# Graph attention and two GCN layers on one core: first loads, checks, result loads, quotients and the order of the last stages rewritten

## The chip, the cores and the metric

The kernel runs on one core of a Trainium2 chip. The metric is device time in microseconds (us) of one execution of the whole program; lower is better. Three executions of the kernel before took 6879.35, 6883.69 and 6887.78 us, so the median is 6883.69 us.

## The reference

The input is x with N = 2708 rows and D = 128 features, and a sparse matrix adj of 2708 x 2708. Everything is float32. With H = 8:

```python
q = (x @ Wq.T).reshape(d, n, h)            # k and v in the same way; d = 128 attentions of width 8
a = einsum('dnh,dmh->dnm', q, k) * scale + adj + adj
out = einsum('dnm,dmh->dnh', softmax(a, axis=2), v).reshape(n, h * d)
x = layernorm(x + out @ Wo.T)
local_hidden = adj @ (x @ W2) + b2
local_cross = adj @ (local_hidden @ W4) + b4
x = layernorm(x + local_cross + local_hidden @ res_w.T + res_b)
```

So there are 128 attentions over 2708 x 2708 positions, each with the same doubled adj added to its scores, and then two products with adj, each reading all of its 29.3 MB.

## The kernel before, in words

**Attention.** Four of the 128 attentions form a group (GB = 4, 32 partitions each), so there are 32 groups g. The query columns are cut into six blocks of 452 (the last has 448), and the key rows into 22 chunks of 128, of which the last is short. For each group and block a plan of nine steps is written out by hand (`interleave`), 1728 steps in all, and the engines run it in that order (`tc.manual_schedule()`, line 313). In a step TensorE forms scores into PSUM (line 438), VectorE adds the adj tile (line 445), ScalarE takes the exponentials (lines 534 and 537), and GpSimd multiplies one chunk's exponentials by exponentials of adj (line 535). TensorE then sums the weighted values (line 463). Projections of x into keys, queries and values go to DRAM (`ks`, `qs`, `vs`) and are read back group by group. Keys and queries are each stored as a high and a low part of 8 rows, so that a group's four attentions occupy 4 x 32 partitions. The sums, eight numerators and one denominator for each position, go to DRAM as `os_`.

**The start.** Lines 369 to 375 load x, the three projection weights and two adj tiles. The first key tile of group 0 comes by 16 transfers of 8 rows (line 254), alternating between the queues of SyncE (SP) and ScalarE, and its queries by 8 transfers of 16 rows (line 287). Line 407 loads the input of the first projection that stands inside the attention.

**Checks.** The attention takes no maxima; a later check decides whether they were needed. `first_exp` (line 413) takes the exponential of adj once in group 0, writes it to DRAM, and has ScalarE add up its elements (`accum_out`). `look_at_near` (line 423) reduces such a tile to its minimum on VectorE, in the last three groups alone. `divide` keeps the smallest and the largest denominator (line 598), and a block at line 652 reduces all these to one number, `n_fine`. After everything, `rest` reads that number (line 721), and a second path runs only if it says so.

**Layer 0's end** (`layer0_out`, line 579). It works on 22 chunks c of 128 rows in an order that is written out. `load(c)` brings a 576 KB tile `ot` of numerators and denominators and a 64 KB tile `xt` of x. `divide(c)` multiplies by reciprocals on VectorE (lines 595 and 600), TensorE transposes eight times (line 603), ScalarE copies. `project(c-1)` multiplies by Wo (line 611), and `add_x(c-2)` adds x and takes statistics. Both load tiles have three buffers. The weights are loaded before this stage (lines 543 to 550). Afterwards the rows are normalised, transposed and multiplied by W2 (lines 632 to 651).

**Layer 1** (`layer1`, line 669). `propagate` sums 22 products of 128 rows into one column block of 512 (six blocks, the last of 148). Each product takes one adj tile of 256 KB from a pool of 24 buffers. The first pass (from line 686) adds b2 and multiplies by W4; the second (from line 694) adds the residual, transposes four pieces, normalises each, and stores each with a transfer on SP's queue (line 705). Here the instructions' order was not written out: a scheduler placed them, and it also placed adj loads of this stage among the loads of layer 0's end.

All loads and stores but the first few stand in one queue, SP's, which issues them in order. SP waits at a transfer until the data or the buffer it needs is there.

Of the kernel before, what the change touches and what calls it, by code (L numbers as in the profile page):

```python
# [9 lines left out]
F32 = mybir.dt.float32  # L10
# [8 lines left out]
P = 128  # L19
# [11 lines left out]
NEAR_LOW = 1e-30  # L31
NEAR_HIGH = 1e18
# [110 lines left out]
def graph_attention_gcn(ctx: ExitStack, tc: tile.TileContext, x, xT, adj, adjT, adjP, adjS,  # L143
# [42 lines left out]
    ends = const.tile([P, 2, len(QBS) * len(TWO_EXP)], F32, name="ends")  # L186


    with ExitStack() as s:
# [58 lines left out]
        def load_keys(g, h, queue=nc.sync):  # L248


            if h == 0:
                groups[g] = kpool.tile([P, NU, P], F32R, tag="k", name="k"), k_short[g % 2], vals[g % 2], v_short[g % 2]
                raw_keys[g] = raw.tile([P, N], F32R, tag="k_raw", name="k_raw")
            queue.dma_start(raw_keys[g][ds(H * h, H), :].bitcast(F32),
                              ks[ds(H * (h % 4 // 2), H), ds((GB * g + h // 4) * N, N)])
# [26 lines left out]
        def load_q(g, b, queues=(nc.sync, nc.sync)):  # L282
            n0, nw = QBS[b]
            q = queries[g, b] = qpool.tile([P, QB], F32R, tag="q", name="q")
            for j in range(GB):
                for i in range(2):
                    queues[i].dma_start(q[ds(32 * j + 2 * H * i, 2 * H), :nw].bitcast(F32),  # L287
                                      qs[:, ds((GB * g + j) * N + n0, nw)])
# [85 lines left out]
        for n in range(2):  # L374
            load_adj(n)

# [20 lines left out]
        for h in range(16):  # L397
            load_keys(0, h, nc.scalar if h % 2 else nc.sync)
# [8 lines left out]
        load_quarter(0)  # L407
# [5 lines left out]
        def first_exp(b, m):  # L413

            nw = QBS[b][1]
            t = ecols.tile([P, QB], F32, tag="ecol", name="ecol")
            x = b * len(TWO_EXP) + TWO_EXP.index(m)
            nc.scalar.activation(t[:, :nw], adj_cols[0, b, -1 - m][:, :nw], AF.Exp, scale=2.0,
                                 accum_out=ends[:, 1, x : x + 1])
            nc.sync.dma_start(near_exp[b, m][:, :nw], t[:, :nw])  # L420
            exp_cols[0, b, m] = t

        def look_at_near(g, b, m):

            x = TWO_EXP.index(m)
            if x % 3 == g - NG + 3:
                nc.vector.tensor_reduce(ends[:, 0, ds(b * len(TWO_EXP) + x, 1)], exp_cols[g, b, m][:, : QBS[b][1]],
                                        AX.X, ALU.min)
# [51 lines left out]
        for what, n, c, beside in interleave(plan, len(steps) // len(plan), NU, amid, bufs=5):  # L480
# [14 lines left out]
            if c == 1 and jobs:  # L495
                jobs.pop(0)()
            if c == 0:
                nq = (g, b + 1) if b + 1 < len(QBS) else (g + 1, 0)
                if i == 3 and nq[0] < NG:
                    load_q(*nq)  # L500

                if g + 1 < NG:
                    t = b * len(plan) + i
                    if t < 32 and t % 2 == 0:
                        load_keys(g + 1, t // 2)
                    elif t < 32 and t % 8 == 7:
                        load_values(g + 1, t // 8)
                    elif 33 <= t < 50 and t % 2:
                        order_keys(g + 1, (t - 33) // 2)
                    elif t >= 50:  # L510
                        spread_values(g + 1, t - 50)
                last = max(loads.index((g, b, x), max(0, loaded - 40)) for x in [chunks_of(p) for p in pieces] + [-1 - two])
                while loaded < min(len(loads), last + 1 + ahead):
                    load_adj(loaded)
                    loaded += 1
                e = epool.tile([P, 8, QB], F32, tag="e", name="e")
                sp = pq.tile([P, 3, NB], F32, tag="p", name="p")
                w = ppool.tile([P, 3, QB], F32, tag="w", name="w")
                if g == 0:
                    first_exp(b, two)  # L520
                at = k = 0
# [10 lines left out]
            if c == len(pieces) - 1:  # L532
                look_at_near(g, b, two)
                nc.scalar.activation(w[:, :, :nw], sp[:, :, :nw], AF.Exp, scale=2.0)  # L534
                nc.gpsimd.tensor_mul(w[:, :, :nw], w[:, :, :nw],  # L535
                                     exp_cols[g, b, two][:, :nw].unsqueeze(1).to_broadcast([P, 3, nw]))
                nc.scalar.activation(e[:, :at, :nw], e[:, :at, :nw], AF.Exp, scale=2.0)  # L537
# [5 lines left out]
    wo = keep.tile([P, H, D], F32, name="wo")  # L543
    nc.sync.dma_start(wo.rearrange("g e f -> g (e f)"), WoT)
    w2, w4, rw = (keep.tile([P, P], F32, name=f"w{i}") for i in range(3))
    for t, src in ((w2, W2), (w4, W4), (rw, res_wT)):
        nc.sync.dma_start(t, src)
    b2_sb, b4_sb, rb_sb, bias = (keep.tile([P, 1], F32, name=f"b{i}") for i in range(4))
    for t, src in ((b2_sb, b2), (b4_sb, b4), (rb_sb, res_b)):
        nc.sync.dma_start(t, src)  # L550
    nc.vector.tensor_add(bias, b4_sb, rb_sb)

# [8 lines left out]
    reach = keep.tile([P, 2, NM], F32, name="reach")  # L561
    nc.gpsimd.memset(reach, 1.0)
    fine = keep.tile([P, 5], F32, name="fine")
# [15 lines left out]
    def layer0_out(sb, ps, pa, judge):  # L579
# [4 lines left out]
        def load(c):  # L584
            i0, w = MC[c]
            ot = sb.tile([P, H + 1, P], F32, tag="ot", name="ot")
            nc.sync.dma_start(ot[:w], o3[ds(i0, w)])
            xt = sb.tile([P, D], F32, tag="xt", name="xt")
            nc.sync.dma_start(xt[:w], x[ds(i0, w), :])
            given[c] = ot, xt  # L590

        def divide(c):
# [3 lines left out]
            if judge:  # L596
                for i, op in enumerate((ALU.min, ALU.max)):
                    nc.vector.tensor_reduce(reach[:w, i, c : c + 1], ot[:w, H, :], AX.X, op)
            on = sb.tile([P, H, P], F32, tag="on", name="on")
            nc.vector.tensor_mul(on[:w], ot[:w, :H, :], rd[:w].unsqueeze(1).to_broadcast([w, H, P]))  # L600
# [17 lines left out]
        load(0)  # L618
        load(1)
        for c in range(NM + 2):  # L620
            if c + 2 < NM:
                load(c + 2)
# [29 lines left out]
        if judge:  # L652
            finite = sb.tile([P, NM * D], F32, tag="finite", name="finite", bufs=1)
            nc.vector.tensor_scalar(finite, ys.rearrange("p c f -> p (c f)"), 0.0, 0.0, ALU.mult, ALU.is_equal)
            nc.vector.tensor_reduce(fine[:, 0:1], finite, AX.X, ALU.min)
            bounds = [(reach[:, 0, :], ALU.min, SUM_LOW, ALU.is_ge), (reach[:, 1, :], ALU.max, SUM_HIGH, ALU.is_le)]
            bounds += [(ends[:, 0, :], ALU.min, NEAR_LOW, ALU.is_ge), (ends[:, 1, :], ALU.max, NEAR_HIGH, ALU.is_le)]
            for i, (a, way, limit, op) in enumerate(bounds):
                end = keep.tile([P, 1], F32, name=f"end{i}")
                nc.vector.tensor_reduce(end, a, AX.X, way)  # L660
                nc.vector.tensor_scalar(fine[:, 1 + i : 2 + i], end, limit, None, op)
            every, ones = (keep.tile([P, 1], F32, name=n) for n in ("every", "ones"))
            nc.vector.tensor_reduce(every, fine, AX.X, ALU.min)
            nc.gpsimd.memset(ones, 1.0)
            pf = pa.tile([P, NB], F32, tag="py", name="pf", bufs=2)
            nc.tensor.matmul(pf[:1, :1], every, ones, start=True, stop=True)
            nc.vector.tensor_copy(n_fine, pf[:1, :1])

    def layer1(s, cols):
# [4 lines left out]
        def propagate(src, n0, nw, last=None):  # L674

            acc = ps.tile([P, NB], F32, tag="wide", name="acc1")
            for m, (m0, mw) in enumerate(MC):
                t = cols.tile([P, NB], F32, tag="col", name="col1")
                nc.sync.dma_start(t[:mw, :nw], adjT[ds(m0, mw), ds(n0, nw)])
                nc.tensor.matmul(acc[:, :nw], src[:mw, m, :], t[:mw, :nw], start=(m == 0),  # L680
                                 stop=(last is None and m == NM - 1))
            if last is not None:
# [3 lines left out]
        for n0, nw in NBS:  # L686
            acc = propagate(xw, n0, nw)
            nc.vector.tensor_scalar(lhT[:, ds(n0, nw)], acc[:, :nw], b2_sb, None, ALU.add)
            for i, w in chunks(nw, P):
# [4 lines left out]
        for n0, nw in NBS:  # L694
            acc = propagate(hw, n0, nw, (rw, lhT[:, ds(n0, nw)]))
            eT = sb.tile([P, NB], F32, tag="eT", name="eT")
            nc.vector.tensor_scalar(eT[:, :nw], acc[:, :nw], bias, None, ALU.add)
            for i, w in chunks(nw, P):
# [7 lines left out]

    def rest(judge):
        with ExitStack() as s:
            cols = s.enter_context(tc.tile_pool(name="cols1", bufs=24))
            with ExitStack() as t:  # L710
# [3 lines left out]
                t.enter_context(tc.manual_schedule())  # L714
                layer0_out(sb, ps, pa, judge)
            layer1(s, cols)
# [136 lines left out]
```

## Time and profile before

| What | us |
|---|---|
| Median of three executions | 6883.69 |
| The profiled execution | 6884.26 |
| Its span, first to last instruction | 6882.5 |
| First score of the attention begins | 41.27 |
| Copy of the last sums begins (line 469) | 6542.98 |
| First and last reciprocal of layer 0's end begin (line 595) | 6553.02 and 6634.42 |
| First product with adj begins (line 680) | 6649.35 |
| Second pass over adj begins | 6764.71 |
| Sixth column block of the second pass begins | 6867.45 |
| Last result store is issued (line 705) | 6877.5 |

The times of single instructions are in us from the span's start. In a timeline line, the columns are start, length, engine, source line, operation, tile written and tile read, shapes, and count; "SPq" is a transfer issued by SP's queue, whose length is that of the issue and not of the transfer. A bracket tells how long the engine had been idle and what ended it. PE is TensorE's matmul stream, PEld its weight loads, DVE VectorE, ACT ScalarE, POOL GpSimd.

### The profile page before, as it was taken

The numbers are of one execution on the slowest core, as the hardware profiler recorded it, in microseconds if no ns is written. First come the engines' busy times: TensorE is split into PE (matmuls) and PEld (weight loads), VectorE is DVE, ScalarE is ACT, GpSimd is POOL, SyncE is SP. The second block draws the span as 40 slices with busy tenths as digits, with TensorE's granted clock in tenths as the row PEclk, the third lists the DMA queues.
The fourth block names the chain that finished last, engine by engine and source line by source line (L and its number), as shares of the span: only waits on it lengthen the run. The fifth ranks groups of instructions, "written<-read, shape, count | busy, mean of one in ns | idle before, by whom it ended". The sixth has DMA issues, their size and how long they took to land.

```text
span 6882.5 us, 138849 instructions
## 1 busy us (share of the span) xinstructions
PE 6655.3 (97%) x50666; PEld 2002.7 (29%) x50666; DVE 6106.7 (89%) x6373; ACT 6505.4 (95%) x3659; POOL 5789.3 (84%) x2706
## 2 busy tenths in 40 slices
PE   7999999999999999999999999999999999999979
PEld 2222222222222222222222222222222222222254
DVE  6899999999999999999999999999999999999941
ACT  7999999999999999999999999999999999999910
POOL 5899988989888899998889999889898898888800
PEclk8999999999999999999999999999999999999999
DMA  8888888778888877788887778887788878777667
GB/s 254 261 250 250 249 244 248 243 246 250 249 254 245 239 245 244 246 251 252 246 243 248 244 240 250 242 253 243 248 251 247 249 233 239 243 233 230 193 204 233
DMA packets 1168590, 1674.27 MB, mean 243 GB/s; under 512 B 153982, under 2 KB 1135954, under 8 KB 1163802
## 3 DMA queue, kind: packets, MB, share of 16 engines
q1 hardware_dynamic: 1167642, 1664.50, 79.0%
q8 instruction: 402, 6.59, 0.4%
q14 instruction: 290, 2.38, 0.1%
q10 hardware_dynamic: 256, 0.81, 0.1%
HBM read 1582.90 MB, written 81.80 MB: 242 GB/s over the span
## 4 chain that ended last, share of the span: by engine, by line
PE 58%; DMA 11%; DVE 11%; POOL 6%; issue 5%; ACT 5%; SPq 4%; DVEq 0%; ACTq 0%; POOLq 0%
PE acc L463 29%; PE s L438 18%; DVE e L445 10%; POOL w L535 6%; DMA col<-in_adjP 4%; PE acc L680 3%; DMA two<-in_adjP 3%; ACT e L537 3%; PE p L438 2%; PE acc L455 2%; SPq L287 2%; ACT w L534 2%; DMA ecol<-ne 2%; PE s L344 1%; PE acc L460 1%
## 5 line engine op out<-in xcount | busy, mean ns | idle before, releaser
L535 POOL TENSOR_TENSOR w<-w,ecol 128x1356 f32<-128x1356 f32 (+1 forms) x1728 | 5347.8, 3102 | 696.1 <-ACT w L534 601.6
L445 DVE TENSOR_TENSOR e<-s,col 128x904 f32<-128x904 f32 (+1 forms) x4608 | 4817.2, 1091 | 320.6 <-PE s L438 130.3
L537 ACT ACTIVATE e<-e 128x2712 f32<-128x2712 f32 (+5 forms) x1728 | 4593.8, 2658 | 9.3 <-DVE e L445 4.3
L463 PE MATMUL acc<-e,vals 128*9 128x452 f32 x20352 | 3561.9, 545 | 0.4 <-ACT e L537 0.4
L438 PE MATMUL s<-q,k 32*128 32x452 f32 x10944 | 2475.2, 462 | 120.9 <-DVE e L445 93.3
L534 ACT ACTIVATE w<-p 128x1356 f32<-128x1356 f32 (+1 forms) x1728 | 2286.0, 1323 | 33.9 <-PE p L438 20.4
L438 PEld LDWEIGHTS s<-q,k 32*128 32x128 f32 x10944 | 997.6, 182 | 3267.6 <-DVE e L445 2845.5
L463 PE MATMUL acc<-w,vals 128*9 128x452 f32 x10368 | 1622.0, 544 | 0.0
L438 PE MATMUL p<-q,k 32*128 32x452 f32 (+1 forms) x5184 | 1328.1, 444 | 21.2 <-ACT w L534 19.6
L445 DVE TENSOR_TENSOR e<-s,two 128x904 f32<-128x904 f32 (+1 forms) x960 | 1048.3, 1092 | 126.5 <-PE s L438 81.3
L463 PEld LDWEIGHTS acc<-e,vals 128*9 128x9 f32 x20352 | 441.7, 88 | 786.2 <-issue 773.7
L438 PEld LDWEIGHTS p<-q,k 32*128 32x128 f32 x5184 | 547.1, 182 | 51.0 <-ACT w L534 45.3
L463 PEld LDWEIGHTS acc<-w,vals 128*9 128x9 f32 x10368 | 207.0, 88 | 175.8 <-issue 160.3
L262 POOL CAST k<-k_raw 128x336 fp32r<-128x336 f32 x251 | 222.2, 886 | 30.1 <-DMA q<-qs 30.1
L460 PE MATMUL acc<-e,v_first 128*32 128x452 f32 (+1 forms) x1536 | 188.9, 564 | 9.8 <-DVE o L469 2.0
L455 PE MATMUL acc<-e,v_short 128*128 128x452 f32 (+1 forms) x384 | 195.1, 590 | 0.0
L344 PE MATMUL s<-wc,xc 128*128 128x256 f32 (+1 forms) x480 | 166.4, 428 | 8.9 <-DMA wc<-in_WkT 7.5
L469 DVE COPY o<-acc 128x452 f32<-128x452 f32 x192 | 119.9, 624 | 40.0 <-PE acc L463 39.8
L360 POOL TENSOR_TENSOR pr<-pa,pr 128x256 fp32r<-128x256 f32 (+1 forms) x160 | 117.8, 736 | 12.8
L346 DVE TENSOR_SCALAR pa<-s 128x256 f32<-128x256 f32 (+1 forms) x240 | 100.2, 418 | 27.6 <-PE s L344 23.9
L344 PEld LDWEIGHTS s<-wc,xc 128*128 128x128 f32 (+1 forms) x480 | 70.5, 184 | 133.4 <-DVE e L445 116.4
L680 PE MATMUL acc<-col,xw 128*128 128x512 f32 (+2 forms) x264 | 106.0, 551 | 0.0
(85 smaller groups left out, 1041.6 us busy)
## 6 DMA issues: line engine op xcount, KB each, us to landing
col<-in_adjP SPq DMA_DIRECT2D x1965, 226.0 KB
two<-in_adjP SPq DMA_DIRECT2D x1440, 226.0 KB
ecol<-ne SPq DMA_DIRECT2D x1395, 226.0 KB
col<-in_adjP SPq DMA_DIRECT2D x393, 224.0 KB
two<-in_adjP SPq DMA_DIRECT2D x288, 224.0 KB
ecol<-ne SPq DMA_DIRECT2D x279, 224.0 KB
col<-in_adjT SPq DMA_DIRECT2D x210, 256.0 KB
k_raw<-ks SPq DMA_DIRECT2D x504, 84.6 KB
```

Of the source, the lines that this page charges most:

```text
L262: copy(k[:, :, ts(i, n)], t[:, ts(i, n * NU)].rearrange("p (q c) -> p c q", c=NU))
L287: queues[i].dma_start(q[ds(32 * j + 2 * H * i, 2 * H), :nw].bitcast(F32), qs[:, ds((GB * g + j) * N + n0, nw)])
L344: nc.tensor.matmul(pp[:mi, 0, :QW], given[c][:, :mi], given.pop((c, i, h)), start=True, stop=True)
L438: nc.tensor.matmul(to[:, :nw], k[r, m, :], q[r], start=True, stop=True)
L445: nc.vector.tensor_add(e[:, ds(at, 2), :nw], st[:, :, :nw], a)
L455: nc.tensor.matmul(a[:, :nw], vz, e[:, t, :nw], start=False, stop=False)
L460: nc.tensor.matmul(a[ds(32 * j, 32), :nw], v_first[g % 2][:, ds(32 * j, 32)], e[:, t, :nw], start=True, stop=False)
L463: nc.tensor.matmul(a[ds(32 * j, VW), :nw], v[:, m, ds(VW * j, VW)], e[:, t, :nw], start=False, stop=(m == last_chunk))
L534: nc.scalar.activation(w[:, :, :nw], sp[:, :, :nw], AF.Exp, scale=2.0)
L535: nc.gpsimd.tensor_mul(w[:, :, :nw], w[:, :, :nw], exp_cols[g, b, two][:, :nw].unsqueeze(1).to_broadcast([P, 3, nw]))
L537: nc.scalar.activation(e[:, :at, :nw], e[:, :at, :nw], AF.Exp, scale=2.0)
L680: nc.tensor.matmul(acc[:, :nw], src[:mw, m, :], t[:mw, :nw], start=(m == 0), stop=(last is None and m == NM - 1))
```

## The change

At the start, keys of group 0 come by 8 transfers of 16 rows, and all its queries by transfers of 8 rows, 16 for each block, in the row order high, high, low, low. The first projection input inside the attention is loaded with the first loads. The sums by ScalarE and the minima by VectorE during the attention are gone; instead VectorE takes the largest absolute value of each adj tile in the first pass over adj, and the denominators are read again as one tile `sums`. The small weights are loaded 40 steps before the attention's end. In layer 0's end the loads are three chunks ahead (four buffers of `ot`, six of `xt`), and three of eight heads are multiplied by GpSimd. Layer 1 now lies in the written order too: pieces of a block's ending wait in a list `due` and are taken up at the products m = 3 and m = 6 of the next block. In the built program SP's queue therefore has, in the second pass, the four stores of a block right behind the adj tile m = 3 of the next block (m = 6 for the first), and all adj loads behind the loads of layer 0's end.

```diff
-    ends = const.tile([P, 2, len(QBS) * len(TWO_EXP)], F32, name="ends")
+    ends = const.tile([P, len(NBS) * NM], F32, name="ends")
+    nc.gpsimd.memset(ends, 0.0)
+    early = ctx.enter_context(tc.tile_pool(name="early", bufs=1))
...
+    def load_weights():
+        nc.sync.dma_start(wo.rearrange("g e f -> g (e f)"), WoT)
+        for t, src in ((w2, W2), (b2_sb, b2), (b4_sb, b4), (rb_sb, res_b)):
+            nc.sync.dma_start(t, src)
...
-            queue.dma_start(raw_keys[g][ds(H * h, H), :].bitcast(F32),
-                              ks[ds(H * (h % 4 // 2), H), ds((GB * g + h // 4) * N, N)])
+            n, parts = (2 * H, 2) if g == 0 else (H, 4)
+            at = 0 if g == 0 else H * (h % 4 // 2)
+            queue.dma_start(raw_keys[g][ds(n * h, n), :].bitcast(F32), ks[ds(at, n), ds((GB * g + h // parts) * N, N)])
...
+            rows, n = ((0, 0, H, H), H) if g == 0 else ((0, 0), 2 * H)
...
+                for i, r in enumerate(rows):
+                    queues[i % 2].dma_start(q[ds(32 * j + n * i, n), :nw].bitcast(F32),
+                                            qs[ds(r, n), ds((GB * g + j) * N + n0, nw)])
...
+        load_quarter(0)
...
-        for h in range(16):
+        for h in range(2 * GB):
             load_keys(0, h, nc.scalar if h % 2 else nc.sync)
...
-        load_quarter(0)
...
-            nc.scalar.activation(t[:, :nw], adj_cols[0, b, -1 - m][:, :nw], AF.Exp, scale=2.0,
-                                 accum_out=ends[:, 1, x : x + 1])
+            nc.scalar.activation(t[:, :nw], adj_cols[0, b, -1 - m][:, :nw], AF.Exp, scale=2.0)
...
+            if n == len(steps) - 40 and c == 0:
+                load_weights()
...
-                look_at_near(g, b, two)
...
-            ot = sb.tile([P, H + 1, P], F32, tag="ot", name="ot")
+            ot = sb.tile([P, H + 1, P], F32, tag="ot", name="ot", bufs=4)
...
-            xt = sb.tile([P, D], F32, tag="xt", name="xt")
+            xt = sb.tile([P, D], F32, tag="xt", name="xt", bufs=6)
...
-            nc.vector.tensor_mul(on[:w], ot[:w, :H, :], rd[:w].unsqueeze(1).to_broadcast([w, H, P]))
+            for multiply, e, n in ((nc.gpsimd.tensor_mul, 5, 3), (nc.vector.tensor_mul, 0, 5)):
+                multiply(on[:w, ds(e, n), :], ot[:w, ds(e, n), :], rd[:w].unsqueeze(1).to_broadcast([w, n, P]))
...
-        load(0)
-        load(1)
+        for c in range(3):
+            load(c)
+        for t, src in ((w4, W4), (rw, res_wT)):
+            nc.sync.dma_start(t, src)
...
+            if c + 3 < NM:
+                load(c + 3)
...
+    def verdict(sb, pa):
+        sums = sb.tile([P, R // P], F32, name="sums", bufs=1)
+        nc.sync.dma_start(sums, os_[H].rearrange("(p n) -> p n", p=P))
...
                 nc.sync.dma_start(t[:mw, :nw], adjT[ds(m0, mw), ds(n0, nw)])
+                if m in (3, 6) and due:
+                    due.pop(0)()
                 nc.tensor.matmul(acc[:, :nw], src[:mw, m, :], t[:mw, :nw], start=(m == 0),
                                  stop=(last is None and m == NM - 1))
+                if look:
+                    x = n0 // NB * NM + m
+                    nc.vector.tensor_reduce(ends[:mw, x : x + 1], t[:mw, :nw], AX.X, ALU.max, apply_absolute_value=True)
...
         for n0, nw in NBS:
-            acc = propagate(xw, n0, nw)
+            acc = propagate(xw, n0, nw, look=judge)
+            take_lh(acc, n0, nw)
+            due.append(lambda n0=n0, nw=nw: form_hw(n0, nw))
+        if judge:
+            due.append(lambda: due.append(verdict(sb, pa)))
...
+        for n0, nw in NBS:
+            acc = propagate(hw, n0, nw, (rw, lhT[:, ds(n0, nw)]))
+            eT = take_e(acc, n0, nw)
+            due.append(lambda eT=eT, n0=n0, nw=nw: put_out(eT, n0, nw))
+        while due:
+            due.pop(0)()
...
         with ExitStack() as s:
+            s.enter_context(tc.manual_schedule())
             cols = s.enter_context(tc.tile_pool(name="cols1", bufs=24))
```

`put_out` does for each of a block's four pieces, one piece after the other: a transpose into one of two PSUM buffers, the addition of x, statistics, a square root on ScalarE, the reciprocal, the scaling, and the store on SP's queue.

## The prediction

> **What bounds the kernel now.** I read the page's busy shares first, then tables by stage, the chain of waits, SP's waits, and the timelines of SP and TensorE.
>
> ```profile
> PE 6655.3 (97%) x50666; PEld 2002.7 (29%) x50666; DVE 6106.7 (89%) x6373; ACT 6505.4 (95%) x3659; POOL 5789.3 (84%) x2706
> 1000.00:2000.00 1000.00, 982.01 (x7666) 282.63 (x7658) 924.57 (x934) 994.95 (x535) 901.60 (x427) 1.00 0.81 248
> 20.00:32.00 12.00, 0.00 (x0) 0.00 (x0) 0.00 (x0) 0.00 (x0) 0.00 (x0) 0.51 0.53 101
> 6610.00:6636.00 26.00, 19.51 (x155) 18.71 (x154) 19.99 (x46) 7.01 (x7) 0.00 (x0) 0.93 0.55 155
> 6766.00:6786.00 20.00, 20.00 (x46) 8.46 (x46) 0.57 (x1) 0.14 (x1) 0.00 (x0) 1.00 1.02 371
> ```
>
> The first line is the page's. The others give window, length, busy time of PE, PEld, DVE, ACT and POOL with counts, granted clock, DMA share and GB/s. Averages mislead here. ScalarE bounds the attention (994.95 of 1000 us). At the start nothing computes and the DMA engines are half used. In layer 0's end TensorE and VectorE alternate, each about three quarters busy. Layer 1 is TensorE's alone: 20.00 of 20, with 371 GB/s behind it.
>
> ```profile
> 17.73 7.41 DMA k_raw<-ks
> 25.17 6.87 DMA k_raw<-ks
> 32.06 0.32 ACTq L287
> ...
> SPq L589 <- DVE st L567: 52.7, 19, 4.3
> SPq L705 <- DVE mv L568: 12.7, 8, 4.3
> SPq L705 <- DVE rs L576: 10.3, 3, 6.2
> SPq L705 <- DVE xo L577: 7.9, 3, 6.8
> ...
> 6765.14 17.19 SPq L679 DMA_DIRECT2D col<-in_adjT  x25
> 6789.19 0.35 SPq L705 DMA_DIRECT2D out<-xo  x1
> ```
>
> The first three lines are the chain at the start: two rounds of key transfers, then the queue. The next four are SP's waits from 6540 on (us in total, times, longest): 52.7 us for buffers of `xt`, and 14 waits in front of result stores. The last two, SP's timeline in the second pass, are the important ones: SP stood from 6782.33 to 6789.19 before a store and issued no adj load. TensorE stayed busy because the stores stood behind tile 18 to 20 of the next block, with many tiles already loaded.
>
> **What the Trainium skill says.** "Perfetto Trace Analysis", section "DMA Instruction — HWDGE (DVE, Sync)": the issuing sequencer waits for a transfer's semaphores before it can go on to the next. The gap just shown agrees. "DMA: Bandwidth & Descriptors", "Rules for kernel authors": a slowest dimension below 16 confines a transfer to that many engines; the DMA share of 0.53 under 8-row transfers agrees. "TensorE: Matmul & The Clock Gate", Part 1: TensorE runs at half rate after an idle window of about 3.4 us, until about 3.4 us of work. Here four transposes took 1.24 us at 6644.69 after 3.27 us idle, and 0.60 at 6652.60. "GPSIMD Engine Reference", section 8: GpSimd shares SBUF interfaces with VectorE, with contention where a VectorE instruction has two SBUF inputs; no line of before shows it for these products.
>
> **The change part by part.** Minus is a gain; brackets hold both ends.
>
> *Keys.* Eight transfers of 16 rows can use all engines: one round, not two. ScalarE works from 32.42, when its queue is through with line 287; a round less is about 7, but 16 query issues instead of 8 stand behind the keys on the two queues (ScalarE's 8 rather than 4, 3.71 us there before in part waiting), so I take 27.6, that is -4.8 (-7 to 0).
>
> *First projection input.* TensorE waited 7.48 for it near 54.9. But the adj tiles behind it land at about 56 anyway, so only SP's two issues (1.18 + 1.24) count: -2.5 (-7.5 to 0). Queries of group 0 take 16 issues per block, not 8; eight took SP 5.43 us at 60.39. Adj loads run 8 tiles ahead and hide most: +2 (0 to +6).
>
> *Attention.* The read of the sum costs 0.09 from start to start (180.22, 180.69, 180.78 on ScalarE), 54 times, on the bounding engine: -4.9 (-5 to 0). The minima are 54 x 0.61 = 33 us of VectorE, but ScalarE was 399.79 busy of 400 beside them: -1 (-4 to 0). The five weight loads near 6392 meet a DMA share of 0.7 and SP's queue: +1 (0 to +4). Start and attention: -10.2.
>
> *Layer 0's end.* Before, the first tile was issued at 6548.30, behind the last stores and weights; now it is ahead of them, near 6543.0. First reciprocal 6547.3 instead of 6553.02: -5.7. Pace: 21 intervals from 6553.02 to 6634.42 are 3.88 each. VectorE's work per chunk was 0.95 + 0.33 (reach) + 1.21 + 0.76 (add, statistics), with overlap 3.13; without reach and with 5/8 of the product it is 2.40. GpSimd's share is 384 elements at 3102 ns for 1356, 0.88 beside it. TensorE: 8 transposes and 8 products, 1.06 + 1.95 = 3.0, now the longest; DMA 640 KB at about 275 GB/s is 2.3. So 3.0 per chunk: 21 x (3.0 - 3.88) = -18.4. With full overlap 2.6 (-27); with contention 3.4 (-10).
>
> *Between.* Five adj products were already done by 6661.6, between the groups of transposes; written order puts them after: +3 (0 to +5). The adj loads start near 6600 and the first product near 6640; 24 tiles, 6.2 MB at 371 GB/s, need 17 us: no loss.
>
> *First pass.* W4 products of a block run at once through two PSUM buffers: 5 x 0.45 = +2.3. The new reductions, 22 x 0.67 = 15 us per block of 20, and `verdict`, some 10 us, lie on a VectorE that worked 0.57 us in 20. They cost nothing unless a tile's reduction delays its buffer, and 24 buffers cover that.
>
> *Second pass, the largest term.* SP now has the four stores directly behind tile m = 3 (m = 6 once). When SP stops there, TensorE has only that tile left. VectorE runs pieces in written order: add 0.29, statistics 0.28, aggregate 0.17, root on ScalarE 0.29, reciprocal 0.16, scaling 0.34. In before's lone piece at 6871.15 the start-to-start steps from statistics to scaling span 1.13; with add and scaling a piece takes 1.71. Four in series: 0.31 + 3 x 1.71 + 1.80 = 7.24. Store 0.38 and load issue put the next tile at 7.75, and an adj load took 2.42 from issue to use at 6420.53: tile 4 is there at about 10.15. TensorE's own work meanwhile is 1.63 (transposes, tile 3): 8.5 lost. Restarting cold, 3.4 us of work at half rate costs +2.5 (1.7 to 3.4 more). Eleven per block, four times 44; in the last block (width 148) products are shorter than SP's 0.38 per issue, so nothing is made up, 12. Together +56 (45 to 68).
>
> *End.* The last two pieces in series: +1.
>
> Sum: -10.2 - 24.1 + 3 + 2.3 + 56 + 1 = +28. The profiled execution took 6884.26 (span 6882.5 and 1.8 around it), 0.6 above the median of 6883.69 and inside the three runs' spread. So 6912.
>
> **Rivals.** About 0.2%, 13.8 us, is what this measurement can tell from no change.
>
> Slower, more strongly: GpSimd and VectorE share the interface and the pace of 3.88 stays. The -18.4 goes: 6930. For it, both operands of the product are in SBUF; against, GpSimd's part is only 0.88.
>
> No change: the stall is half as large, 28 instead of 56, because the scheduler's pieces overlap more than I allow or the clock doesn't drop: 6884. Against it, VectorE's order is written and the reciprocal must wait for ScalarE's root. The forecast turns to "same" below 42 us of total stall, 8.4 per block.
>
> Faster: the stores don't hold back the loads behind them, and only the gains are left: 6884 - 10 - 24 + 6 = 6856. One mechanism decides, whether SP stands at a store. Against it, SP's 14 waits at line 705; for it, those never emptied TensorE. A cheaper chain alone (below 5 us in all for four pieces) would already bring it near no change.
>
> **How the numbers follow.** Forecast 0.70; slower rival 0.08; same 0.12; faster 0.10. The unknown ends of pace (-9 to +8), stall (-11 to +12) and the start, combined, give 6891 to 6938; this holds the slower rival too and leaves out the two others. So slower 0.78, same 0.12, faster 0.10.
>
> **What would show it.** Right: SP's timeline of the second pass shows four stores, then the adj loads of m = 4 and on; TensorE is idle some 7 to 9 us in each of five blocks, waiting for an adj tile, with a granted clock below 1 after it; the second pass takes about 165 us instead of 6764.71 to 6873.9, 109. First exponential near 27.6; first reciprocal near 6547 and then one every 3.0 us, with GpSimd's part of the product under 1.3. Wrong: a second pass below 130 us; a pace above 3.5; waits of TensorE for `col` in the first pass, which would say that the reductions hold the buffers; or a start not earlier than 41.27 for the first score.

## The result, and the profile after

The changed kernel took 6940.19 us (median of four executions, 6933.89 to 6943.9), the kernel before 6885.73 (6879.35 to 6888.31): a ratio of 1.0078, 95% interval 1.0066 to 1.0091. That is 54 us slower; 28 were forecast, and the time lies 2 us above the stated range. The profiled execution took 6943.2 (span 6941.4).

Where the two profiled executions differ, by stage (us; minus is earlier or shorter):

| Stage | Before | After | Difference | Forecast |
|---|---|---|---|---|
| Start to copy of the last sums | 6542.98 | 6550.9 | +7.9 | -10.2 |
| from there to the first reciprocal | 10.0 | 4.8 | -5.2 | -5.7 |
| 21 intervals of reciprocals | 81.4 | 63.3 | -18.1 | -18.4 |
| last reciprocal to first adj product | 14.9 | 30.8 | +15.9 | +5.3 with the next |
| first pass over adj | 114.8 | 110.6 | -4.2 | |
| second pass over adj | 109.7 | 170.6 | +60.9 | +56 |
| what follows it | 8.5 | 10.3 | +1.8 | +1 |

The second pass is counted from its first product, at 6764.18 before.

The changed kernel's page and windows for the same places as before (columns as there), of which the third lies in layer 0's end; the last line is the same window of the kernel before:

```profile
PE 6691.3 (96%) x50666; PEld 2020.7 (29%) x50666; DVE 6148.1 (89%) x6405; ACT 6500.8 (94%) x3605; POOL 5822.0 (84%) x2728
```

```profile
20.00:32.00 12.00, 0.00 (x0) 0.00 (x0) 0.00 (x0) 0.00 (x0) 0.31 (x1) 0.55 0.89 112
1000.00:2000.00 1000.00, 980.47 (x7661) 281.32 (x7653) 923.53 (x933) 993.12 (x536) 900.11 (x428) 1.00 0.81 245
6575.00:6601.00 26.00, 25.25 (x215) 23.62 (x214) 21.21 (x43) 9.12 (x9) 14.19 (x9) 1.00 0.79 216
...
6575.00:6601.00 26.00, 18.03 (x153) 16.87 (x151) 20.91 (x47) 6.31 (x7) 0.00 (x0) 1.00 0.94 275
```

The page's shares hardly move, though 59 us were lost. At the start the DMA engines are now busier (0.89 instead of 0.53) and yet move 112 GB/s instead of 101. The middle of the attention is unchanged. In layer 0's end TensorE, busy 18.03 of 26 before, is busy 25.25 of 26.

Three views of the second pass follow: SP's timeline, TensorE's timeline, and waits of SP and TensorE from 6540 on (total, times, longest).

```profile
6789.00 5.29 SPq L723 DMA_DIRECT2D out<-xo  x4
6794.38 10.98 SPq L682 DMA_DIRECT2D col<-in_adjT  x19
6819.26 5.47 SPq L723 DMA_DIRECT2D out<-xo  x4
```

```profile
6789.39 1.02 PE L685 MATMUL acc<-col,hw 128*128 128x512 f32 x2
6797.30 8.01 PE L685 MATMUL acc<-col,hw 128*128 128x512 f32 x11 [6.89 <-DMA col<-in_adjT]
```

```profile
SPq L723 <- DVE y L720: 75.5, 16, 13.9
```

```profile
PE acc L685 <- DMA col<-in_adjT: 35.4, 6, 6.9
PE pe L718 <- DVE y L720: 8.2, 10, 1.4
```

Read them together. Before, SP's stop at a store left TensorE many tiles. Here SP can issue the next adj load only at 6794.38, behind the fourth store; TensorE ends its last tile at 6790.4 and stands 6.89 us. The eleven matmuls that follow take 8.01 us; at the pace before, 14.00 us for 32 at 6661.56, they would take 4.8: the slow clock. SP's waits in front of stores grew from 33.3 in all (30.9 in the three lines shown of before) to 84.4 in all (75.5 in the line shown). The whole stage, per window (length, busy times of PE, PEld, DVE, ACT, POOL, clock, DMA share, GB/s):

```profile
6786.00:6819.00 33.00, 23.34 (x50) 9.45 (x48) 6.62 (x26) 1.47 (x5) 0.00 (x0) 0.84 0.44 152
```

A stretch in which TensorE was busy 20.00 of 20 us, at a granted clock of 1.00 and 371 GB/s, has become one of 23.34 in 33, at 0.84 and 152 GB/s.

### The profile page after: what moved, and what is told of

Read it like the earlier page. It is cut to its first block, busy times and chain, and to the rows that moved or that the text cites. A ratio compares the mean times of both kernels' runs of the same rounds, so it can differ in the third digit from the quotient of the medians.

```text
span 6941.4 us, 138959 instructions
## 1 busy us (share of the span) xinstructions
PE 6691.3 (96%) x50666; PEld 2020.7 (29%) x50666; DVE 6148.1 (89%) x6405; ACT 6500.8 (94%) x3605; POOL 5822.0 (84%) x2728
## 5 line engine op out<-in xcount | busy, mean ns | idle before, releaser
L541 ACT ACTIVATE e<-e 128x2712 f32<-128x2712 f32 (+5 forms) x1728 | 4653.2, 2693 | 13.3 <-DVE e L448 8.9
L538 ACT ACTIVATE w<-p 128x1356 f32<-128x1356 f32 (+1 forms) x1728 | 2345.7, 1357 | 31.6 <-PE p L441 28.2
L441 PE MATMUL p<-q,k 32*128 32x452 f32 (+1 forms) x5184 | 1319.5, 445 | 30.8 <-ACT w L538 28.2
L685 PE MATMUL acc<-col,hw 128*128 128x512 f32 (+2 forms) x264 | 118.2, 604 | 35.4 <-DMA col<-in_adjT 35.4
```

Of the source, the lines that this page charges most:

```text
L441: nc.tensor.matmul(to[:, :nw], k[r, m, :], q[r], start=True, stop=True)
```

## Experiments

Each experiment changes the changed kernel, unless it says "before". Since executions differ by some us in the attention, I also compare traces at single steps of it: "step n" is the start of ScalarE's n-th of 1728 exponentials of line 538 (534 before), given relative to the first trace of the kernel before. A gain in us of the whole is worked out from the ratio to the kernel before.

### The second pass

**Stores on ScalarE's queue.**

```diff
-                nc.sync.dma_start(out[ds(n0 + i, w), :], o[:w])
+                nc.scalar.dma_start(out[ds(n0 + i, w), :], o[:w])
```

> The changed kernel, with the result stores of the second pass issued by ScalarE's queue instead of SP's. Theory (SP stands at the four stores and so starves TensorE): TensorE's waits for adj tiles in the second pass (35.4 us in the changed kernel) go, and most of the 13 us of slow clock with them; the waits inside the pieces, 8 to 10 us, stay. Second pass 120 to 130 us instead of 170, total about 6894 (6885 to 6905). Rival (the pieces in TensorE's own order, with the clock that they let fall, are the loss): second pass still 150 or more, total 6920 to 6940.

Measured: 6893.44, ratio to before 1.0010 (1.0004 to 1.0017). SP's timeline has no stop left, and the same window of TensorE shows it:

```profile
6755.69 112.68 SPq L682 DMA_DIRECT2D col<-in_adjT  x125
```

```profile
6786.00:6819.00 33.00, 29.99 (x72) 13.11 (x73) 10.12 (x40) 2.36 (x8) 0.00 (x0) 1.00 0.85 280
```

SP issues 125 adj loads without a store between them. The second pass takes 121 us, no wait for `col` is left in it, the waits inside the pieces stay at 8.2, and the clock is back at 1.00.

**Stores later on SP's own queue.**

```diff
+        def store():
+            while given:
+                nc.sync.dma_start(*given.pop(0))
...
+                if m == 18:
+                    store()
                 if m in (3, 6) and due:
...
-                o = sb.tile([P, D], F32, tag="xo", name="xo")
+                o = sb.tile([P, D], F32, tag="xo", name="xo", bufs=6)
...
-                nc.sync.dma_start(out[ds(n0 + i, w), :], o[:w])
+                given.append((out[ds(n0 + i, w), :], o[:w]))
```

Since a finished piece is now kept longer, its tile `xo` has six buffers instead of three.

> The changed kernel with the stores still on SP's queue, but put off to behind adj tile m = 18 of the next block; the pieces' computation stays at m = 3 (m = 6 for the first). Theory (place of the stores in the queue is what matters): as with the stores on ScalarE's queue, 6894 (6885 to 6905). Rival (a store on SP's queue costs, wherever it is): within 10 us of the changed kernel, 6930 to 6940.

Measured: 6895.66, ratio 1.0013 (1.0006 to 1.0020). SP still stands in front of the first store here, from 6781.74 to 6787.69, but TensorE has its tiles; one wait for `col` is left in the second pass:

```profile
PE acc L691 <- DMA col<-in_adjT: 2.9, 1, 2.9
```

So it is neither the queue nor the store that costs, but what stands behind the store: 47 and 45 us (of 6940.19) are won by two different mends of the same wait. The theory holds, the rivals fall.

### Start and group 0

**Keys and queries as before.**

```diff
-            n, parts = (2 * H, 2) if g == 0 else (H, 4)
+            n, parts = H, 4
...
-            rows, n = ((0, 0, H, H), H) if g == 0 else ((0, 0), 2 * H)
+            rows, n = (0, 0), 2 * H
```

> The changed kernel with group 0's keys again in 16 transfers of 8 rows and its queries in 8 transfers of 16 rows per block. Theory (16 query transfers per block hold SP's queue up, and ScalarE with it, by more than 2 us per block): first score stays at 41 to 42, and from step 3 to step 54 of the attention ScalarE no longer falls behind; 13 to 18 us less, about 6925 (6921 to 6929). Rival (the early projection input or the missing sums shift the loads, and queries cost 2 us in all): 6935 to 6942.

Measured: 6939.31, ratio 1.0082 (1.0065 to 1.0098): nothing won. The trace shows two things that nearly cancel. From step 3 to step 54 ScalarE falls back by 3.0 us instead of 13.3, so the query transfers do cost. But the first score comes at 45.97 and not at 41 to 42, step 0 is 4.6 us later and step 3 is 7.4 later; 2.9 us are left at step 54. The 4.6 are those of one pair of traces; how far a start varies by itself is seen below.

**First projection input where it was.**

```diff
             load_adj(n)
-        load_quarter(0)
...
             project_all(1, i)()
+        load_quarter(0)
```

> The changed kernel with the first projection input loaded where it was before, behind the start's loads. Theory (the early load stands ahead of the keys and costs what the single round of keys gains): first score near 37 instead of 41.3, then TensorE waits some 7 us for the input, as before; at step 54 of the attention within 1 us of the changed kernel, total 6936 to 6943. Rival (start time is set by the 16 query transfers): first score stays at 41 to 42, and step 3 of the attention is 7 us later than in the changed kernel; by step 54 it is 0 to 2 us later.

Measured: 6938.44, ratio 1.0077 (1.0060 to 1.0093). First score at 41.3; step 3 is 6.1 us later than in the changed kernel, step 6 equal, step 54 1.6 later. The rival holds: beside the changed queries the early load is worth 6 us for three steps, nothing at step 6 and 1.6 at step 54, and it is not what sets the first score.

ScalarE's queue at the start of the changed kernel tells what does:

```profile
16.10 2.96 ACTq L266 DMA_DIRECT2D k_raw<-ks  x4
22.29 10.40 ACTq L299 DMA_DIRECT2D q<-qs  x8
```

The keys' second round is gone, as forecast, and its time is filled by a queue that is busy with eight query issues until 32.69, where before it was free at 32.42.

**All of group 0's loads as before; and the kernel before once more.**

> The changed kernel with keys, queries and first projection input of group 0 all as before, so that only ScalarE's sums and VectorE's minima are missing from the attention. Theory (the sums' 0.09 x 54 on the bounding engine are won whole): step 54 of the attention at 278.2 (before: 283.1), total 6931 to 6934. Rival (in group 0 a faster ScalarE only meets its adj tiles earlier): step 54 at 280.5 or later, with waits of ScalarE for adj tiles, total 6935 or more.

> The kernel before, unchanged, for a second trace of it. Theory (the 5.7 us by which the changed kernel falls behind between steps 54 and 1572 of the attention belong to it): ScalarE's steps in the two traces of the kernel before stay within 1.5 us of each other over that stretch. Rival (they are one execution's own): they drift apart by 3 us or more.

Measured: 6936.70, ratio 1.0069 (1.0052 to 1.0086), step 54 at 290.4; and a single execution of the kernel before at 6895.82. This second trace of before starts at 47.3 instead of 44.1 and reaches step 54 7.7 us later, without any change. My number for the rival (280.5 or later) was thus no test: I had taken one trace's start for the kernel's. Against the second trace, from step 6 to step 54, the kernel without sums gains 3.4 us, most of the 4.3 that 48 x 0.09 gives; against the first it gains nothing, so these traces don't settle what the sums cost. Between steps 54 and 1572 the second trace of before falls 1.4 us behind the first, and changed kernels range from 1.3 ahead to 7.6 behind: this slow drift stays without a cause.

Taken over all traces, the starts part more clearly. In the five with the old keys and queries (these two runs, the first of before, the run above with old keys and queries, and the first of the next set) the first exponential comes at 44.1 to 48.8 us, 46.8 on average; in the thirteen with the new ones at 43.0 to 45.4, 44.3 on average. So the new keys win some 2.5 us at step 0, and the first trace of before was an early one. The early input, too, can be seen beside the old keys and queries: with it step 3 comes 7.6 us earlier than in the run without it, step 6 4.9 and step 54 4.3 earlier, but the medians (6939.31 and 6936.70) show no gain.

**From the other side: the kernel before with single parts of the change.** The first run drops `accum_out` and `look_at_near`; the second has the changed keys, queries and early input, as in the diff above; the third has all of them.

```diff
-            nc.scalar.activation(t[:, :nw], adj_cols[0, b, -1 - m][:, :nw], AF.Exp, scale=2.0,
-                                 accum_out=ends[:, 1, x : x + 1])
+            nc.scalar.activation(t[:, :nw], adj_cols[0, b, -1 - m][:, :nw], AF.Exp, scale=2.0)
...
-                look_at_near(g, b, two)
```

> The kernel before without ScalarE's sums of the adj exponentials and without VectorE's minima of them (this part of its verdict is left out). Theory (both stand on the path: 4.9 us of ScalarE in group 0, and about 4 us in the last three groups, where all traces of changed kernels gain 3 to 5.5 us between steps 1572 and 1727): about 6877 (6874 to 6880), ratio about 0.9987. Rival (ScalarE only meets its loads earlier): 6883 to 6888.

> The kernel before with the changed start alone: keys of group 0 in 8 transfers of 16 rows, queries in 16 transfers of 8 rows per block, first projection input with the first loads. Theory (what keys and input gain, the query transfers of the first six blocks give back, 2 us a block): within 3 us of the kernel before, 6883 to 6889. Rival (as I forecast, 5 us are won): 6879 to 6882. Second rival (queries cost more than the start gains): 6890 or more.

> The kernel before with both: the changed start, and neither ScalarE's sums nor VectorE's minima (that part of its verdict is left out). Theory (the two add: 6.6 us won by the one, 3.7 lost by the other): 6883 to 6887. Rival (they interact: a ScalarE without sums only meets the query transfers, and the gain of the sums is lost): 6888 to 6893, and then the attention's missing 5 us are explained.

Measured: 6881.01, ratio 0.9989 (0.9980 to 0.9997), 7.6 us won; 6891.33, ratio 1.0007 (0.9999 to 1.0015), about 5 us lost, a time in the second rival's range, though not apart from no change; 6885.87, ratio 0.9998 (0.9989 to 1.0006). Within this noise the parts add. The forecast of 5 us won by the start is the one that fell. The first run's trace tells where its gain lies: from step 6 to step 54, where the sums are gone, 0.8 us against the first trace of before and 4.1 against the second; from step 1656 to the end, where the minima are gone, 7.4 and 8.9.

**What in the query transfers costs: their number or their 8 rows.** The start stores a second copy `qx` of the queries in the order low, high, so that from the second block on 8 transfers of 16 rows do again; the second run cuts each of them in half along the columns (the lines with `cuts`).

```diff
+                    src = qx if g == 0 and b > 0 and i else qs
+                    cuts = ((0, nw // 2), (nw // 2, nw)) if g == 0 and b > 0 else ((0, nw),)
```

> The changed kernel with one mend: from the second block on, the queries of group 0 come in 8 transfers of 16 rows, half of them from a second copy in the order low, high that the start stores (1 MB). Theory (the 16 transfers a block hold the attention up): between steps 6 and 36 ScalarE falls 4 us behind the kernel before instead of 9.4; total about 6935 (6932 to 6937). Rival (what holds it up is the adj tiles' own rate): still 8 us or more, total 6938 to 6943.

> The same, but each of the 8 transfers is cut into two of half the columns: 16 issues a block again, each of 16 rows. Theory A (the number of issues in SP's queue costs): between steps 6 and 36 8 us or more behind, total 6938 to 6943, as the changed kernel. Theory B (transfers of 8 rows cost, whatever their number): 4 us behind, total 6932 to 6937, as with 8 issues.

Measured: 6937.73, ratio 1.0069 (1.0057 to 1.0081); and 6952.24, ratio 1.0093 (1.0080 to 1.0106). ScalarE's waits for adj tiles between 60 and 215 us, of the two in turn:

```profile
ACT ecol L439 <- DMA col<-in_adjP: 8.6, 6, 2.3
```

```profile
ACT ecol L441 <- DMA col<-in_adjP: 16.1, 7, 4.2
```

From step 6 to step 36 ScalarE falls back 6.3 us with 8 issues, 12.9 with 16 issues of 16 rows, and 9.4 in the changed kernel with 16 issues of 8 rows. The ten traces with 16 issues of 8 rows range from 7.9 to 12.5 here, and those with 8 issues of 16 rows from 0 to 6.3. Cutting the same transfers in halves costs 6.6 us by the steps and 14.5 by the medians, so 16 rows don't help if the issues double. The number of issues in SP's queue is the likely reason; but halves also double the number of pieces of memory that are moved, each half as long, and no run parts the two. The 6952 lie above the ranges of both theories. The gain of 8 issues was smaller than expected (3 us by the steps), and the medians don't part it from the changed kernel.

**Weights after the attention.**

```diff
-            if n == len(steps) - 40 and c == 0:
-                load_weights()
...
+        load_weights()
         for t, src in ((w4, W4), (rw, res_wT)):
```

> The changed kernel with Wo and the small weights loaded behind the first three result tiles of layer 0's end, not in the attention. Theory (40 steps before the end they cost the attention about 1 us): within 3 us of the changed kernel, attention's end at most 1 us earlier. Rival (they hold up adj tiles and are the attention's missing 5 us): attention's end 4 to 6 us earlier.

Measured: 6939.67, ratio 1.0075 (1.0062 to 1.0087). The attention ends 5.2 us earlier, and the place is exact: relative to step 1656, the changed kernel is 0.65 us ahead of before at step 1688 and 3.31 behind at step 1690; with the weights moved it is 0.78 ahead at 1690, and the two stay 4.4 apart until the end. SP's timeline of the changed kernel at that place:

```profile
6389.56 0.33 SPq L194 DMA_DIRECT2D wo<-in_WoT  x1
6389.94 0.42 SPq L196 DMA_DIRECT2D w<-in_W  x1
6390.41 0.90 SPq L196 DMA_DIRECT2D b<-in_b  x2
6391.36 0.43 SPq L196 DMA_DIRECT2D b<-in_res_b  x1
```

Five issues, 2.2 us of SP's queue and 576 KB, ahead of the adj tiles that ScalarE needs next. The median of the whole doesn't show this gain, so I take the 4.4 us for the place alone.

### Layer 0's end

**All quotient products on VectorE; the same with two chunks ahead and three buffers.**

```diff
-            for multiply, e, n in ((nc.gpsimd.tensor_mul, 5, 3), (nc.vector.tensor_mul, 0, 5)):
-                multiply(on[:w, ds(e, n), :], ot[:w, ds(e, n), :], rd[:w].unsqueeze(1).to_broadcast([w, n, P]))
+            nc.vector.tensor_mul(on[:w], ot[:w, :H, :], rd[:w].unsqueeze(1).to_broadcast([w, H, P]))
```

```diff
-            ot = sb.tile([P, H + 1, P], F32, tag="ot", name="ot", bufs=4)
+            ot = sb.tile([P, H + 1, P], F32, tag="ot", name="ot")
...
-            xt = sb.tile([P, D], F32, tag="xt", name="xt", bufs=6)
+            xt = sb.tile([P, D], F32, tag="xt", name="xt")
...
-            if c + 3 < NM:
-                load(c + 3)
+            if c + 2 < NM:
+                load(c + 2)
```

> The changed kernel with all eight quotient products of a chunk on VectorE. Theory (without the two reductions VectorE needs 0.95 + 1.21 + 0.76 = 2.9 us, less than TensorE's 3.0): reciprocals 3.0 to 3.1 us apart, total within 4 us of the changed kernel, 6936 to 6944. Rival (GpSimd's share is what made the pace): reciprocals 3.4 to 3.9 apart, total 6948 to 6960.

> The changed kernel with all quotient products on VectorE and with layer 0's end loaded two chunks ahead from three buffers, as before: of the changes to this stage, the two reductions' absence and the order of SP's queue are left. Theory (VectorE's work per chunk was the limit): reciprocals at most 3.2 us apart, total 6936 to 6945. Rival (SP's waits for the buffers of x, 52.7 us before, set the pace): reciprocals 3.6 to 3.9 apart, total 6950 to 6960.

Measured: 6939.85, ratio 1.0079 (1.0062 to 1.0096), reciprocals 3.03 apart; and 6956.96, ratio 1.0099 (1.0084 to 1.0115), 3.67 apart. SP's and VectorE's waits in this stage, with the old buffers; the last line is VectorE's with the new ones, from the first run:

```profile
SPq L584 <- DVE st L562: 63.8, 19, 7.7
```

```profile
DVE rd L590 <- DMA ot<-os: 19.1, 18, 4.2
...
DVE rd L590 <- DMA ot<-os: 4.8, 3, 4.3
```

GpSimd's share is worth nothing; the depth of the loads is worth 13.4 us (21 x 0.64); what is left, 21 x (3.88 - 3.67) = 4.4, belongs to the two reductions that are gone and to the new order of SP's queue, which no run parts. VectorE waits 4.8 us for `ot` instead of 19.1. For the depth the rival was right.

### Between the layers

**Transposes of the next group ahead of the W2 products.**

```diff
-        for c0 in range(0, NM, 4):
+        def turn(c0):
...
+        def times(c0, cs, parts, x1T):
...
+        held = turn(0)
+        for c0 in range(0, NM, 4):
+            now, held = held, turn(c0 + 4) if c0 + 4 < NM else None
+            times(c0, *now)
```

`turn` is the first half of the loop's body (normalise, transpose, copy), `times` the second (products with W2, copy). The transposes' PSUM tile now takes turns between two buffers.

> The changed kernel with the transposes of the next group of four chunks placed ahead of the W2 products of the present group. Theory (between layer 0 and layer 1 TensorE runs at half clock because each group leaves it idle): eight W2 products of a full group take 1.16 us instead of 2.08 from the second or third group on, and the first adj product comes 12 to 14 us after the first transpose instead of 20.7; about 7 us less, 6933 (6930 to 6937). Rival (the copies on ScalarE set the pace): the products stay at 2.08, 17 us or more from first transpose to first adj product, total 6936 to 6940.

Measured: 6933.50, ratio 1.0066 (1.0049 to 1.0083); from first transpose to first adj product 12.75 us instead of 20.65. TensorE's timeline of the changed kernel, and of this one:

```profile
6634.72 2.08 PE L645 MATMUL pw<-w,x1T 128*128 128x128 f32 x8 [0.68 <-ACT x1T L642]
6638.32 2.08 PE L645 MATMUL pw<-w,x1T 128*128 128x128 f32 x8 [0.67 <-ACT x1T L642]
```

```profile
6634.14 1.93 PE L648 MATMUL pw<-w,x1T 128*128 128x128 f32 x8
6636.74 1.16 PE L648 MATMUL pw<-w,x1T 128*128 128x128 f32 x8
```

The same eight products take 2.08 us in every group of the changed kernel and 1.16 here from the second group on, as the theory says. But this run alone doesn't show that the order is the reason. In the run with the first input moved back, whose instructions in this stage are those of the changed kernel, they fall to 1.16 at the second group as well:

```profile
6630.82 2.08 PE L645 MATMUL pw<-w,x1T 128*128 128x128 f32 x8 [0.68 <-ACT x1T L642]
6634.43 1.16 PE L645 MATMUL pw<-w,x1T 128*128 128x128 f32 x8 [0.68 <-ACT x1T L642]
```

There the first adj product comes 15.27 us after the first transpose. Of eleven traces with the groups one after the other, nine kept 2.08 in all full groups, one left it at the second group and one at the third; both traces with the transposes ahead (this one and the last version below) left it at the second. So the order alone wins 2.5 us (15.27 to 12.75), and it probably helps the clock, which gives the rest.

### A version that beats both

Four mends together: stores on ScalarE's queue, pieces of a block taken up one by one (m in 3, 6, 9, 12, 15), transposes ahead, and the query copy.

> The changed kernel with four mends: stores of the second pass on ScalarE's queue; the pieces of a block's ending taken up one by one at tiles m = 3, 6, 9, 12 and 15; transposes of the next group ahead of the W2 products; and queries of group 0 after the first block in 8 transfers of 16 rows, from a second copy of them in the order low, high that the start stores. From the changed kernel's 6940: second pass -58 (stall, slow clock, most of TensorE's waits for pieces), transposes -7, queries about -8: 6867 (6858 to 6876), under the kernel before's 6886. Rival (the query copy's stores and the ScalarE queue cost what they save): 6876 to 6890.

Measured: 6866.92, ratio to before 0.9972 (0.9961 to 0.9983). A window of its second pass:

```profile
6760.00:6793.00 33.00, 33.00 (x83) 13.86 (x82) 9.61 (x34) 1.77 (x6) 0.00 (x0) 1.00 0.91 309
```

TensorE is busy in all of it; the second pass takes 110 us, as before, and what layer 0's end won is kept.

## Why the prediction was wrong, point by point

The direction and the main mechanism were right, the size was half. The terms come to (single edits where there are any, else the profiled pair):

| Term | Forecast | Measured | By |
|---|---|---|---|
| keys, first input, queries | -4.8 - 2.5 + 2 = -5.3 | +5 (-1 to +10) | the new start on before |
| sums, minima | -4.9 - 1 = -5.9 | -7.6 (-14 to -2) | before without them |
| weights in the attention | +1 | +4.4 | steps around 1690 |
| layer 0's end | -24.1 | -23.3 | the profiled pair |
| between, first pass | +5.3 | +11.7 | the profiled pair |
| second pass, end | +57 | +62.7 | the profiled pair |
| sum | +28 | +53 | median: +54 |

That the sum meets the median so closely is in part luck: the first two rows are known to some 6 us each, and the profiled pair alone gives +7.9 for start and attention, where the first three rows give +1.8.

ScalarE's waits between 60 and 215 us, the costliest line each of before, of the changed kernel, and of the changed kernel with old keys and queries; the first point rests on them:

```profile
ACT w L534 <- PE s L438: 8.0, 1, 8.0
...
ACT ecol L429 <- DMA col<-in_adjP: 11.7, 6, 4.2
...
ACT ecol L429 <- DMA col<-in_adjP: 6.8, 4, 2.6
```

- **The failed step: "Eight transfers of 16 rows can use all engines: one round, not two ... -4.8", and queries "+2".** A round of keys did go, but in the first block 16 query issues filled its time (read from the queue's timeline, not tried alone), so that 2.5 us or so were won, and in the next five blocks they held SP up. On the kernel before, keys, first input and queries together lost about 5 us instead of winning 5.3. "Adj loads run 8 tiles ahead and hide most" was wrong. In the lines above, the wait that stems from the first projection input is gone with the change, and waits for adj tiles stand in its place. They are 11.7 us with all edits, 6.8 with the old keys and queries, 7.7 with only the first input moved back and 0.3 with both, so the early input on the one hand and the new keys and queries on the other each bring such waits. In group 0, SP also holds a store for each exponential and waits for ScalarE there (25.2 us in before's trace from 60 to 400, 15.0 after), so it can't run ahead; that this is why the cover fails is argued from these waits and was not tried alone.
- **First input "-2.5".** Beside the changed queries it won 6 us at step 3 and nothing by step 6; beside the old ones 4.3 us at step 54. No median shows a gain. The argument (the adj tiles behind it decide) fits this.
- **Weights "+1 (0 to +4)"** and **minima "-1 (-4 to 0)"** both fell outside their ranges. From step 1656 to the end, the kernels with neither minima nor early weights gain some 7.4 us on before's first trace and 8.9 on its second. Taking ScalarE's 399.79 of 400 for proof of cover was the error: from 5990 on, before still had waits of ScalarE of 4.3 us, which the kernel without minima hasn't; the other 3 us stay open. **Sums "-4.9"**: the traces give 0.8 or 4.1, depending on which trace of before is taken. That sums and minima together came near the forecast is thus luck.
- **Pace of layer 0's end "3.0 per chunk".** The number was right, and so was TensorE as the limit that is left, but what had held the pace at 3.88 was not. I let VectorE's lighter work bring TensorE's 3.0 through; the run with the old buffers has no reductions and stays at 3.67. The line I had quoted, SP's 52.7 us of waits for the buffer of `xt`, was most of the cause. That the loads were made deeper in the same change is why the number came out. GpSimd's part of the product took 1.59, over the 1.3 that I had named as a sign.
- **"Between ... +3" and "+2.3".** Too small by 6.4. I had counted matmuls at full clock; in written order each group leaves TensorE idle for 0.7 us, and the clock stayed low for all six groups. In the run with the first input moved back, where it rose at the second group, this stretch and the first pass are 5.6 us shorter, which is nearly the whole miss. The Trainium skill ("TensorE: Matmul & The Clock Gate", Part 1) asks for about 3.4 us of sustained work until the full rate comes back; between two gaps TensorE worked 2.9 us here (6631.11 to 6634.04), so the slow 20 us agree with it, and I had overlooked the gaps. Two runs with the same gaps left the slow rate all the same, so the gaps alone don't decide. The new reductions cost nothing, as forecast: in the first pass TensorE waited for no adj tile.
- **Second pass "+56 (45 to 68)": +61.** The chain of a piece was 1.65 us (1.71 forecast), waits were 35.4 + 8.2, which is 8.7 a block (8.5 forecast), and the slow clock added 118.2 - 104.9 = 13.3 us of matmul time over the first pass, 2.7 a block (2.5 forecast). SP at the stores is shown by two mends.
- **The rivals** all fell: contention doesn't set layer 0's pace, the stall was not halved, and stores do hold back the loads.

The predicted upper end, 6938, was too low because it combined the unknown ends of pace, stall and start alone. The terms between the layers, over by 6.4, and of the weights, over by 3.4, were not in it, and the keys had no loss side at all.

## What to carry to other kernels

A store in an in-order load queue costs what stands behind it: place it where the consumer still has more loaded than the store's producer needs time, or give it another queue. Halving the rows of transfers to use all engines in one place doubled the issues in another; count issues per queue where that queue has no slack. And where one engine is busy nearly all the time, as ScalarE in this attention, small things that delay its inputs can be on the path, as five weight loads were here with 4.4 us: test such edits from both sides, on the old kernel and on the new one.

## What the runs showed of the hardware

- TensorE's low clock lasted 20 us while it was idle for only 0.7 of each 3.6 us, and whether it ends differs between executions of the same instructions: with all quotient products on VectorE eight W2 products fell from 2.08 to 1.16 at the third group, with the first input moved at the second, in the changed kernel never.
- After the four stalls of 6.8 to 6.9 us in the second pass's wide blocks, TensorE's products followed one another slowly, mostly every 0.85 us instead of every 0.43, for 6.1, 3.4, 6.1 and 4.2 us. So the same stall cost 1.7 to 3.1 us of clock within one execution.
- GpSimd's product of 128 x 384 elements took 1.59 us beside VectorE, not the 0.88 worked out from its rate in the attention; VectorE's part of 640 took 0.82, where its share of 1.21 is 0.76. The slowdown lies with GpSimd (by its span, and its reason was not tried), and costs nothing here.
- The same kernel's first exponential came at 44.1 and at 47.3 us in two executions, so one trace's start is good to some 3 us only.
